# A shared expert's last quarter in units of 512 tokens instead of 256, at other places between the routed experts

## The chip, the cores and the metric

The kernel runs on one core of a Trainium2 chip. The time is the device time of one execution in microseconds, smaller is better: a median of 2704.23 us over three runs (2700.75 to 2708.0). The engines are TensorE (PE, matmuls; PEld, its weight loads), VectorE (DVE), ScalarE (ACT), GpSimd (POOL) and SyncE (SP). SP and POOL issue the DMAs; each engine takes its instructions in a fixed order that was settled when the program was built.

## The reference, cut to what matters

A decoder layer on 4096 tokens of width 512: an attention-like block, a cross attention, then a feed-forward part with one shared expert and 32 routed ones (top 1). Only the last part is touched:

```python
x = hidden_states.reshape(-1, 512)                       # 4096 tokens
shared_out = (silu(x @ shared_gate_w) * (x @ shared_up_w)) @ shared_down_w    # inner width 1024
logits = x @ gate_w                                       # 32 experts
topk_ids = argmax(logits, -1); scores = sigmoid(max(logits, -1))
xs = x * scores
# each token by its own expert e: (silu(xs @ gate[e]) * (xs @ up[e])) @ down[e]
return shared_out + routed_out
```

All is float32. The kernel keeps that precision with split operands: `split` makes a high part (a cast on ScalarE to TensorE's reduced float32) and a low part (the difference, on VectorE unless told otherwise), and every product of two split operands is three matmuls (`three`: low by high, high by low, high by high).

## The kernel before, in words

**Stages.** `build` runs stage0 (first block), stage1 (cross attention, normalisation, gate, the transposed and split tokens `zT` in DRAM), `shared`, `routed` and `overflow` (a loop for experts with more tokens than their place allows; its count is read from the plan). Written in one program, they overlap at their seams: a planner orders each engine's instructions at build time by their place in the program and by a timeline that it computes, gives tiles free buffers of their tag, and adds the waits.

**Shared expert.** Its inner width is 1024. `shared` does the first 768 (three pairs of 256), and writes the sum with the residual plainly to `out`. The last 256 are the class `Rest`, in units of tokens, and stand between the routed experts: a unit's `load` brings its tokens `z` (high and low) from `zT`; `gate` and `up` make the products with the resident weights; `down` makes the outputs, which are copied to a tile `v` and added to `out` by an accumulating DMA from POOL. A unit of 256 tokens has 24 matmuls of 256 columns in gate, 24 in up, and 12 of 512 columns in down.

**Routed experts.** `routed` takes them by rank: `CAP` gives the room of each rank (448, 384, five of 256, four of 192, thirteen of 128, eight of 64 tokens); which expert holds a rank is read at run time from `plan`. An expert's tokens are cut into blocks of 256, 128 and 64. `gather` fetches rows of `xs` by index, `turn` transposes them on TensorE, gate and up are made by `hidden` (256) or `gate`/`up` (128, 64), `down` scatters its outputs with an accumulating indirect DMA (L1331). Each expert has 24 weight pieces of 128 x 512 (eight each for gate, up, down), loaded by SP (L1185) to one of 14 landing buffers (six of tag "raw", eight of tag F, in a fixed cycle) and split (L94 on ACT, L97 on DVE) into tiles of W (45, gate and up) or A and B (eight each, down).

**The order.** The list `blocks` decides. Before the change it begins with shared unit 0, and one further unit follows each expert whose room isn't 128, as long as there are any. With S for shared units and rank:tokens for the routed blocks:

```
S0 0:256 0:128 0:64 S1 24:64 S2 11:128 1:256 1:128 S3 25:64 S4 12:128 2:256 S5 26:64 S6 13:128 3:256 S7
27:64 S8 14:128 4:256 S9 28:64 S10 15:128 5:256 S11 29:64 S12 16:128 6:256 S13 30:64 S14 17:128 7:128 7:64
S15 31:64 18:128 8:128 8:64 19:128 20:128 9:128 9:64 21:128 22:128 10:128 10:64 23:128
```

For block i the loop writes down, in this order: `prepare` of block i+2 (its z or its gather), the next expert's gate weights, the gate of i, the transposes, the next expert's up weights, the up of i, and then the down of block i-1, with the down weights of the expert that follows that block's expert. (For a block of 256, "gate" and "up" are the two halves of `hidden`.) So a block's down stands behind the whole gate and up of the next block. The z of unit 0 is loaded at the end of `shared`.

**Buffers that the change touches.** z: tag E, four tiles, all four for one unit. s: G (four). The split hidden values: C and D (six each). v: I (two). Banks of PSUM: P1 (down, and the transposes of blocks under 256), P2 (gate), P3 (up), P4, two of each.

Of the kernel before, what the change touches and what calls it, by code (L numbers as in the profile page):

```python
# [8 lines left out]
F32 = mybir.dt.float32  # L9
FR = mybir.dt.float32r  # L10
# [4 lines left out]
A = mybir.AluOpType  # L15
AF = mybir.ActivationFunctionType
# [5 lines left out]
T = 4096  # L22
C = 512
E = 32
# [5 lines left out]
CAP = [448, 384] + [256] * 5 + [192] * 4 + [128] * 13 + [64] * 8  # L30
# [11 lines left out]
def f32(ap):  # L42
    return ap.bitcast(F32)
# [45 lines left out]
def split(g, hi, lo, src, lo_engine=None, hi_engine=None):  # L89

    if isinstance(lo_engine, cycle):
        lo_engine = next(lo_engine)
    if hi_engine is None:
        g.nc.scalar.copy(hi, src)  # L94
    else:
        hi_engine.tensor_copy(hi, src)
    g.low = (lo_engine or g.nc.vector).tensor_tensor(lo, src, f32(hi), A.subtract)  # L97
# [22 lines left out]
def part(w, k, c):  # L120

    return w[k][c // 4][:, c % 4 * 128:c % 4 * 128 + 128]
# [40 lines left out]
def three(terms):  # L163

    (wh, wl), (xh, xl) = terms
    return (wl, xh), (wh, xl), (wh, xh)
# [199 lines left out]
def place(t):  # L366

    at = t // 4 * 4 + t % 2 * 2 + t % 4 // 2
    return slice(at * 256, at * 256 + 256)


def stage1(g, x1, mask, kst, vst, gate, x2, zT, zF, xs, ef, background):
    nc = g.nc
    NT = T // 256
# [534 lines left out]
def shared(g, zT, zF, x2, out, pairs, wd, routing, rest, rest_weights):  # L909
# [129 lines left out]
    for n, (G, p) in enumerate(steps):  # L1039
        last = n + 1 == len(steps)  # L1040
        if p == PAIRS - 2 and G + 1 < NG:
            parts = sums(g, zF, G + 1, SUM, nc.gpsimd)
        wn = {}
        ahead = rest_weights if last else pairs.steps(steps[n + 1][1], wn)
        behind = down_weights(g, wd, p, w)
        more = pairs.sums(2) if n == 0 else None

        def between(a):
            next(ahead, None)
            if len(before) < 5:  # L1050
                next(behind, None)
            if parts:
                next(parts, None)
            if p == PAIRS - 1 and G + 1 < NG:
                Z[a] = load_z(g, zT, SUM, G + 1, a, nc.gpsimd)
            if before:
                before.pop(0)()
            if more:
                next(more, None)
            next(routing, None)  # L1060

        up(G, p, w, between)
        while before:
            before.pop(0)()
        for _ in ahead:
            pass
        before = [lambda a=(G, p, w, half, s): down(*a) for half in (1, 0) for s in range(4)]
        w = wn
# [19 lines left out]
class Rest:  # L1088
# [5 lines left out]

    def load(self, b):
        g, nc = self.g, self.g.nc
        z = []
        for c in range(2):
            z.append([])
            for i in range(2):  # L1100
                v = g.tile("E", "z", FR, (128, 2, 256))
                nc.sync.dma_start(f32(v[:]), self.zT[i, :, 2 * c:2 * c + 2, place(b)])
                z[c].append(v)
        self.Z[b] = z

    def product(self, b, which, tag):
        g, nc = self.g, self.g.nc
        p = g.bank(tag, which, (128, 2, 256))
        for i in range(2):
            n = 0  # L1110
            for k in range(4):
                for w, x in three((g.rest[which], self.Z[b][k // 2])):
                    nc.tensor.matmul(p[:, i, :], part(w, k, i), x[:, k % 2, :], start=n == 0, stop=n == 11)
                    n += 1
        return p

    def gate(self, b):
        g, nc = self.g, self.g.nc
        p = self.product(b, "g", "P2")
        s = g.tile("G", "s", F32, (128, 2, 256))  # L1120
        nc.scalar.activation(s[:], p[:], AF.Silu)
        self.S[b] = s

    def up(self, b):
        g, nc = self.g, self.g.nc
        p = self.product(b, "u", "P3")
        s = self.S.pop(b)
        nc.vector.tensor_tensor(s[:], p[:], s[:], A.mult)
        hh, hl = g.tile("C", "hh", FR, (128, 2, 256)), g.tile("D", "hl", FR, (128, 2, 256))
        split(g, hh[:], hl[:], s[:])  # L1130
        self.H[b] = hh, hl
        del self.Z[b]

    def down(self, b):
        g, nc = self.g, self.g.nc
        h = self.H.pop(b)
        for j in range(2):
            o = g.bank("P1", "d")
            n = 0
            for k in range(2):  # L1140
                for w, y in three((g.rest["d"], h)):
                    nc.tensor.matmul(o[:], y[:, k, j * 128:(j + 1) * 128], w[k][0], start=n == 0, stop=n == 5)
                    n += 1
            v = g.tile("I", "v")
            nc.scalar.copy(v[:], o[:])
            nc.gpsimd.dma_start(self.out[b * 256 + j * 128:b * 256 + j * 128 + 128, :], v[:], accum_op=A.add)

def routed(g, xs, rest, plan, idx, wg, wu, wd, out):  # L1150
    nc = g.nc
# [84 lines left out]
    def up_product(b, r, which, tag):  # L1236
        hi, lo = W[r][which]
        for n in range(2):
            p = g.bank(tag, which)
            product(p, [(X[b], k) for k in range(4)], [(hi[2 * k + n], lo[2 * k + n]) for k in range(4)])  # L1240
            yield p
# [90 lines left out]
                                         in_=v[rows], in_offset=None, bounds_check=T - 1, oob_is_err=False, compute_op=A.add)  # L1332


    left = [(b, None, 256) for b in range(T // 256)]
    blocks = [left.pop(0)]
    for r in order:
        at = 0
        while at < CAP[r]:
            m = next(m for m in (256, 128, 64) if at + m <= CAP[r])  # L1340
            blocks.append((BASE[r] + at // 128, r, m))
            at += m
        if CAP[r] != 128 and left:
            blocks.append(left.pop(0))
    blocks += left
    nxt = dict(zip(order, order[1:]))
# [16 lines left out]
    def second(b, r, m):  # L1363
        if r is None:
            rest.up(b)
        elif m < 256:
            up(b, r, m)
        else:
            hidden(b, r, 1)

    def third(b, r, m):
        if r is None:
            rest.down(b)
        else:
            down(b, r, m)
# [13 lines left out]
    for w in "gud":  # L1389
        load(order[0], w)  # L1390
    for i, block in enumerate(blocks):
        b, r, m = block
        last = r is not None and (i + 1 == len(blocks) or blocks[i + 1][1] != r)
        if i + 2 < len(blocks):
            prepare(*blocks[i + 2])
        if last and r in nxt:
            load(nxt[r], "g")
        first(*block)
        if i + 1 < len(blocks):
            turn_x(*blocks[i + 1])  # L1400
        if i > 0:
            turn_hidden(*blocks[i - 1])
        if last and r in nxt:
            load(nxt[r], "u")
        second(*block)
        if i > 0:
            third(*blocks[i - 1])
            r = blocks[i - 1][1]
            if r != block[1] and r in nxt:
                load(nxt[r], "d")  # L1410
# [64 lines left out]
def build(tc, I, out):  # L1475
    from contextlib import ExitStack
    nc = tc.nc
    with ExitStack() as outer:
# [14 lines left out]
        with ExitStack() as inner:  # L1493
            g = Ctx(tc, inner)
            g.ident = ident[:]
            g.mhalf = g.c.tile([128, 8], F32, name="mhalf")
            nc.gpsimd.memset(g.mhalf[:], -0.5)
            ef = g.c.tile([128, E], F32, name="ef")
            idx = g.c.tile([128, NB], I32, name="idx")
            with later(g, 20):  # L1500
                nc.sync.dma_start(ident[:], I["ident"])
                empty = g.tile("A", "empty", I32, (128, NBLK))
                nc.gpsimd.memset(empty[:], T)
                for v in lists:
# [50 lines left out]
```

## Time and profile before

| | |
|---|---|
| median of three runs | 2704.23 us (2700.75 to 2708.0) |
| the profiled execution, time and span | 2703.28 us, 2701.4 us |
| granted TensorE clock, mean over the span | 0.997 |
| busy: PE, DVE, ACT, POOL | 2641.7, 2071.4, 1853.0, 1132.2 us |
| first and last gate matmul of the shared units (L1113) | 1798.3 us, 2472.2 us |
| start of rank 0's first product | 1825.8 us |
| start of the last matmul | 2690.9 us |
| bytes moved by DMA | 446.66 MB |

All places in time are microseconds from the start of the span of one profiled execution. "PE L1113 MATMUL g<-z,rw" is a matmul issued by line 1113 that writes a tile named g from tiles z and rw. Matmuls are pipelined: the duration of one is longer than the distance to the next. In a list of waits a row names the waiting engine and line, what it waited for, and the total, the number and the longest of these waits.

### The profile page before, as it was taken

The numbers are of one execution on the slowest core, as the hardware profiler recorded it, in microseconds if no ns is written. First come the engines' busy times: TensorE is split into PE (matmuls) and PEld (weight loads), VectorE is DVE, ScalarE is ACT, GpSimd is POOL, SyncE is SP. The second block draws the span as 40 slices with busy tenths as digits, with TensorE's granted clock in tenths as the row PEclk, the third lists the DMA queues.
The fourth block names the chain that finished last, engine by engine and source line by source line (L and its number), as shares of the span: only waits on it lengthen the run. The fifth ranks groups of instructions, "written<-read, shape, count | busy, mean of one in ns | idle before, by whom it ended". The sixth has DMA issues, their size and how long they took to land. (4 is left out here: it accounts for less than half of the span.)

```text
span 2701.4 us, 47562 instructions
## 1 busy us (share of the span) xinstructions
PE 2641.7 (98%) x14629; PEld 2274.0 (84%) x14629; DVE 2071.4 (77%) x4703; ACT 1853.0 (69%) x4118; POOL 1132.2 (42%) x911
## 2 busy tenths in 40 slices
PE   7999999999999999999999999999999999999998
PEld 5878888887878999899997878778989898898886
DVE  7777777777777988888887487574777777778985
ACT  7788788888767777677785323343666676767885
POOL 5576565666644334344341457621122222212221
PEclk9999999999999999999999999999999999999999
DMA  4012112212021223323249846663889899999994
GB/s 154 32 63 86 55 67 81 81 47 76 30 87 34 80 76 130 103 92 107 79 143 338 289 142 238 218 211 108 261 282 281 281 305 299 295 284 291 323 319 148
DMA packets 269408, 446.66 MB, mean 165 GB/s; under 512 B 33536, under 2 KB 77568, under 8 KB 269152
## 3 DMA queue, kind: packets, MB, share of 16 engines
q1 hardware_dynamic: 254464, 416.46, 45.5%
q0 software_dynamic: 14688, 27.17, 4.9%
q8 instruction: 115, 1.88, 0.3%
q14 instruction: 141, 1.16, 0.1%
HBM read 348.83 MB, written 96.64 MB: 165 GB/s over the span
## 5 line engine op out<-in xcount | busy, mean ns | idle before, releaser
L97 DVE TENSOR_TENSOR rl<-raw,rh 128x512 fp32r<-128x512 f32 x768 | 487.7, 683 | 86.8 <-ACT rh L94 59.6
L94 ACT CAST rh<-raw 128x512 fp32r<-128x512 f32 x768 | 438.3, 621 | 138.5 <-DMA raw<-in_rg 89.2
L97 POOL TENSOR_TENSOR pl<-p,ph 128x512 fp32r<-128x512 f32 x320 | 411.3, 1296 | 263.2 <-ACT ph L94 206.5
L349 ACT ACTIVATE rl<-s 128x512 f32<-128x512 f32 x512 | 293.0, 604 | 38.1 <-PE s L345 32.8
L1331 POOL DMA_INDIRECT out_dram<-v,idx x46 | 114.7, 2492 | 457.7 <-ACT v L1329 367.4
L464 ACT ACTIVATE e<-e,nm 128x128 f32<-128x128 f32 x512 | 199.2, 391 | 70.4 <-DVE nm L461 70.1
L353 DVE TENSOR_TENSOR p<-s,rl 128x512 f32<-128x512 f32 x320 | 215.0, 682 | 40.6 <-ACT rl L349 38.2
L94 ACT CAST ph<-p 128x512 fp32r<-128x512 f32 x320 | 199.2, 626 | 63.1 <-DVE p L353 60.2
L467 POOL TENSOR_TENSOR e<-e,ri 128x512 f32<-128x512 f32 x128 | 133.2, 1042 | 215.0 <-DVE ri L465 103.3
L345 PE MATMUL s<-qh,kwl 128*128 128x512 f32 x512 | 205.7, 403 | 7.3 <-DVE p L353 4.1
L309 PE MATMUL o<-pl,vwh 128*128 128x512 f32 x512 | 202.8, 396 | 1.4 <-POOL pl L97 1.4
L309 PE MATMUL o<-ph,vwl 128*128 128x512 f32 x512 | 200.4, 393 | 0.9 <-ACT ph L94 0.9
L353 DVE TENSOR_TENSOR s<-s,rl 128x512 f32<-128x512 f32 x192 | 133.2, 694 | 88.3 <-ACT rl L349 87.8
L345 PE MATMUL s<-ql,kwh 128*128 128x512 f32 x512 | 200.1, 391 | 0.0
L345 PE MATMUL s<-qh,kwh 128*128 128x512 f32 x512 | 199.9, 390 | 0.0
L309 PE MATMUL o<-ph,vwh 128*128 128x512 f32 x512 | 199.7, 390 | 0.0
L970 PE MATMUL gu<-z,swh 128*128 128x512 f32 x504 | 157.3, 389 | 0.0
L438 PE MATMUL q<-yh,wql 128*128 128x256 f32 x512 | 149.5, 292 | 2.8 <-DVE v L497 2.4
L97 DVE TENSOR_TENSOR pl<-s,ph 128x512 fp32r<-128x512 f32 x192 | 131.0, 683 | 20.6 <-ACT ph L94 18.2
L438 PE MATMUL q<-yh,wqh 128*128 128x256 f32 x512 | 145.6, 284 | 0.0
L438 PE MATMUL q<-yl,wqh 128*128 128x256 f32 x512 | 145.0, 283 | 0.0
L97 POOL TENSOR_TENSOR vl<-v,vh 128x512 fp32r<-128x512 f32 x64 | 84.4, 1319 | 124.3 <-ACT vh L94 111.6
(361 smaller groups left out, 7996.1 us busy)
## 6 DMA issues: line engine op xcount, KB each, us to landing
raw<-in_rg SPq DMA_DIRECT2D x256, 256.0 KB
raw<-in_ru SPq DMA_DIRECT2D x256, 256.0 KB
raw<-in_rd SPq DMA_DIRECT2D x256, 256.0 KB
z<-zT SPq DMA_DIRECT2D x116, 256.0 KB
b<-x SPq DMA_DIRECT2D x40, 256.0 KB
raw<-in_sgu SPq DMA_DIRECT2D x39, 256.0 KB
swh<-wS SPq DMA_DIRECT2D x36, 256.0 KB
swl<-wS SPq DMA_DIRECT2D x36, 256.0 KB
```

The costliest lines, as they stand in the source:

```text
L94: g.nc.scalar.copy(hi, src)
L97: g.low = (lo_engine or g.nc.vector).tensor_tensor(lo, src, f32(hi), A.subtract)
L309: nc.tensor.matmul(o[:], w, y[:], start=kt == 0 and n == 0, stop=kt == 15 and n == 2)
L345: nc.tensor.matmul(s[:], w, y[:], start=n == 0, stop=n == 2)
L349: m0 = nc.scalar.activation(r[:], s[:], AF.Relu)
L353: m1 = nc.vector.tensor_tensor(p[:], s[:], r[:], A.mult)
L438: nc.tensor.matmul(o[:, i, :], part(w, k, p), y[k // 2][:, k % 2, :], start=n == 0, stop=n == 11)
L464: nc.scalar.activation(e[:, hs], e[:, hs], AF.Exp, bias=nm[:, h:h + 1], scale=0.125, accum_out=su[:, h:h + 1])
L467: nc.gpsimd.tensor_tensor(e4, e4, ri[:].unsqueeze(2).to_broadcast([128, 4, 128]), A.mult)
L970: nc.tensor.matmul(o[:], y, z, start=(at, x) not in begun, stop=j == 1 and m == 2, skip_group_check=True)
L1331: nc.gpsimd.indirect_dma_start(out=out, out_offset=bass.IndirectOffsetOnAxis(ap=idx[rows, b + j:b + j + 1], axis=0), in_=v[rows], in_offse ...
```

## The change

The 4096 tokens go through `Rest` in eight units of 512 instead of sixteen of 256. A unit's z is eight tiles of 128 x 512, four of tag E (high) and four of tag F (low). Gate and up each fill two banks (one for each 128 of the 256 inner columns) with matmuls of 512 columns; each bank has its own Silu, product and split. Down has four outputs of 128 tokens instead of two. The rows of `out` follow from the order in which `zT` holds the tokens. In the list of blocks, a unit follows an expert only if its room is over 128 and under 384, and one unit is always kept back, so that the last block is a shared unit:

```
S0 0:256 0:128 0:64 24:64 11:128 1:256 1:128 25:64 12:128 2:256 S1 26:64 13:128 3:256 S2 27:64 14:128 4:256 S3
28:64 15:128 5:256 S4 29:64 16:128 6:256 S5 30:64 17:128 7:128 7:64 S6 31:64 18:128 8:128 8:64 19:128 20:128
9:128 9:64 21:128 22:128 10:128 10:64 23:128 S7
```

A side effect of the loop's rule for down weights: where a unit stood between two experts, the second one's down weights were asked for with that unit; where it is gone, they are asked for after the gate and up weights of the expert behind.

```diff
     def load(self, b):
-        z = []
-        for c in range(2):
-            z.append([])
+        self.Z[b] = z = []
+        for k in range(4):
+            z.append([g.tile("EF"[i], "z", FR) for i in range(2)])
             for i in range(2):
-                v = g.tile("E", "z", FR, (128, 2, 256))
-                nc.sync.dma_start(f32(v[:]), self.zT[i, :, 2 * c:2 * c + 2, place(b)])
-                z[c].append(v)
-        self.Z[b] = z
+                nc.sync.dma_start(f32(z[k][i][:]), self.zT[i, :, k, b * 512:(b + 1) * 512])
 
     def product(self, b, which, tag):
-        p = g.bank(tag, which, (128, 2, 256))
         for i in range(2):
+            p = g.bank(tag, which)
             n = 0
             for k in range(4):
-                for w, x in three((g.rest[which], self.Z[b][k // 2])):
-                    nc.tensor.matmul(p[:, i, :], part(w, k, i), x[:, k % 2, :], start=n == 0, stop=n == 11)
+                for w, x in three((g.rest[which], self.Z[b][k])):
+                    nc.tensor.matmul(p[:], part(w, k, i), x[:], start=n == 0, stop=n == 11)
                     n += 1
-        return p
+            yield p
 
     def gate(self, b):
-        p = self.product(b, "g", "P2")
-        s = g.tile("G", "s", F32, (128, 2, 256))
-        nc.scalar.activation(s[:], p[:], AF.Silu)
-        self.S[b] = s
+        self.S[b] = []
+        for p in self.product(b, "g", "P2"):
+            s = g.tile("G", "s")
+            nc.scalar.activation(s[:], p[:], AF.Silu)
+            self.S[b].append(s)
 
     def up(self, b):
...
+        for s, p in zip(self.S.pop(b), self.product(b, "u", "P3")):
+            nc.vector.tensor_tensor(s[:], p[:], s[:], A.mult)
+            hh, hl = g.tile("C", "hh", FR), g.tile("D", "hl", FR)
+            split(g, hh[:], hl[:], s[:])
+            self.H[b].append((hh, hl))
 
     def down(self, b):
-        for j in range(2):
+        for s in range(4):
             o = g.bank("P1", "d")
             n = 0
             for k in range(2):
-                for w, y in three((g.rest["d"], h)):
-                    nc.tensor.matmul(o[:], y[:, k, j * 128:(j + 1) * 128], w[k][0], start=n == 0, stop=n == 5)
+                for w, y in three((g.rest["d"], h[k])):
+                    nc.tensor.matmul(o[:], y[:, s * 128:(s + 1) * 128], w[k][0], start=n == 0, stop=n == 5)
                     n += 1
             v = g.tile("I", "v")
             nc.scalar.copy(v[:], o[:])
-            nc.gpsimd.dma_start(self.out[b * 256 + j * 128:b * 256 + j * 128 + 128, :], v[:], accum_op=A.add)
+            at = (b // 2 * 4 + s // 2 * 2 + b % 2) * 256 + s % 2 * 128
+            nc.gpsimd.dma_start(self.out[at:at + 128, :], v[:], accum_op=A.add)
...
-    left = [(b, None, 256) for b in range(T // 256)]
+    left = [(b, None, 512) for b in range(T // 512)]
     blocks = [left.pop(0)]
     for r in order:
...
-        if CAP[r] != 128 and left:
+        if 128 < CAP[r] < 384 and len(left) > 1:
             blocks.append(left.pop(0))
     blocks += left
```

More of the change, by code (lines that the diff above doesn't have):

```diff
@@ L1096, in load @@
         g, nc = self.g, self.g.nc
-        z = []
-        for c in range(2):
-            z.append([])
+        self.Z[b] = z = []
+        for k in range(4):
+            z.append([g.tile("EF"[i], "z", FR) for i in range(2)])
             for i in range(2):
-                v = g.tile("E", "z", FR, (128, 2, 256))
-                nc.sync.dma_start(f32(v[:]), self.zT[i, :, 2 * c:2 * c + 2, place(b)])
-                z[c].append(v)
-        self.Z[b] = z
+                nc.sync.dma_start(f32(z[k][i][:]), self.zT[i, :, k, b * 512:(b + 1) * 512])
     def product(self, b, which, tag):
         g, nc = self.g, self.g.nc
-        p = g.bank(tag, which, (128, 2, 256))
         for i in range(2):
+            p = g.bank(tag, which)
             n = 0
             for k in range(4):
-                for w, x in three((g.rest[which], self.Z[b][k // 2])):
-                    nc.tensor.matmul(p[:, i, :], part(w, k, i), x[:, k % 2, :], start=n == 0, stop=n == 11)
+                for w, x in three((g.rest[which], self.Z[b][k])):
+                    nc.tensor.matmul(p[:], part(w, k, i), x[:], start=n == 0, stop=n == 11)
                     n += 1
-        return p
+            yield p
     def gate(self, b):
         g, nc = self.g, self.g.nc
-        p = self.product(b, "g", "P2")
-        s = g.tile("G", "s", F32, (128, 2, 256))
-        nc.scalar.activation(s[:], p[:], AF.Silu)
-        self.S[b] = s
+        self.S[b] = []
[3 more added lines that the diff above has]
+            self.S[b].append(s)
     def up(self, b):
         g, nc = self.g, self.g.nc
[L1126 to L1131, printed above, removed]
+        self.H[b] = []
+        for s, p in zip(self.S.pop(b), self.product(b, "u", "P3")):
[3 more added lines that the diff above has]
+            self.H[b].append((hh, hl))
         del self.Z[b]
```

## The prediction

> **What bounds the kernel now.** I read the page's engine totals first, then the busy time by stretch for the part that the change touches (from about 1800 us to the end), then TensorE's waits there, its order of time, and last what feeds it. The stretches, one row each: length, busy time of every engine with its instruction count, granted clock, DMA share, GB/s.
>
> ```profile
> PE 2641.7 (98%) x14629; PEld 2274.0 (84%) x14629; DVE 2071.4 (77%) x4703; ACT 1853.0 (69%) x4118; POOL 1132.2 (42%) x911
> ...
> 1900.00:2480.00 580.00, 579.03 (x3517) 517.87 (x3516) 434.31 (x707) 403.90 (x754) 130.98 (x86) 1.00 0.91 286
> 2480.00:2660.00 180.00, 179.66 (x852) 148.33 (x851) 164.11 (x273) 149.34 (x284) 48.38 (x22) 1.00 0.94 316
> ```
>
> TensorE is busy 579.03 of 580 and 179.66 of 180 us. A busy TensorE need not be at its peak, so I look at its waits between 1850 and 2690 us (total, times, longest), which are all of them:
>
> ```profile
> PE g L1288 <- ACT th L94: 1.0, 2, 0.6
> PE d L1233 <- ACT th L94: 0.5, 1, 0.5
> PE d L1142 <- DVE tl L97: 0.3, 1, 0.3
> PE d L1233 <- DVE tl L97: 0.2, 1, 0.2
> ```
>
> Two microseconds in 840, and the clock is 1.00. So in the routed stage the time is the number of matmuls times the distance of their starts. Close behind stand the DMA engines (0.91 to 0.94) and, after 2480 us, VectorE (164 of 180 us). That is narrow enough that I must ask at each moved step whether the weights still come in time.
>
> **Step 1: 512 columns instead of 256 in gate and up.** Per pair of old units the change replaces 96 matmuls of 256 columns by 48 of 512; the 24 down matmuls of 512 columns stay. In all, 768 matmuls of 256 become 384 of 512. Their distance is read from the order of time, not from the mean durations (283 and 390 ns, which overlap):
>
> ```profile
> 2086.09 0.39 PE L1142 MATMUL d<-rdh,hl 128*128 128x512 f32 x1
> 2086.31 0.39 PE L1142 MATMUL d<-rdh,hh 128*128 128x512 f32 x1
> 2086.54 3.04 PE L1113 MATMUL g<-z,rw 128*128 128x256 f32 x24
> 2089.41 0.60 PE L1204 MATMUL pt<-ident,x 128*128 128x128 f32 x4
> ```
>
> 512 columns: starts 0.227 us apart (2086.31 to 2086.54). 256 columns: 24 matmuls start from 2086.54 on and the next operation begins at 2089.41, so 2.87 / 24 = 0.120 us. Before: 768 x 0.120 = 92.2 us; after: 384 x 0.227 = 87.2 us. **Gain 5.0 us.** The Trainium skill speaks against this gain: "TensorE: Matmul & The Clock Gate", section "Back-to-back issue gap", gives N / 2.4 + 2.5 ns, that is 109.2 and 215.8 ns, hence 768 x 0.1092 - 384 x 0.2158 = 1.0 us only. The row shows 120 and 227, further from the rule for the short one, and I take the row; 1.0 us stays as the lower end. Weight loads halve too (768 to 384), but they overlap.
>
> ScalarE, VectorE and the bytes don't change: per 512 tokens there are still two Silu, two products, two splits, four copies and 2 MB of z, now with 2 KB runs. All these are under TensorE's cover.
>
> **Step 2: the end.** Today the last product of expert rank 23 is followed by one copy and one scatter:
>
> ```profile
> 2691.41 0.59 ACT L1329 COPY v<-d 128x512 f32<-128x512 f32 x1 [5.88 <-issue]
> ...
> 2692.27 1.56 POOL L1331 DMA_INDIRECT out_dram<-v,idx  x1 [5.42 <-ACTq L1420]
> ```
>
> The last matmul starts at 2690.94; the scatter's issue ends at 2693.83, 2.9 us later; 7.6 us more to the end of the span at 2701.4. After the change, rank 23's down comes ahead of the last shared unit's down (24 x 0.227 = 5.4 us, four outputs). The accumulating DMA of a shared unit waits until the scatter before it has landed:
>
> ```profile
> 2006.87 1.89 POOL L1146 DMA_DIRECT2D out_dram<-v  x2 [6.78 <-DMA out_dram<-v,idx]
> ```
>
> and v has two buffers (tag I). Counted from M, the start of rank 23's last matmul: copy to M+1.06, scatter issued M+1.33 to 2.89. Landing: M+5.9 (near the 2.9 us that pass at the end of the trace between the scatter's issue and the release at 2696.8; 6.8 after issue when DMA is crowded; "DMA: Bandwidth & Descriptors", section "Anatomy of one DMA - SWDGE (gpsimd) path", would give 2.0 us + 0.6 for 256 KB, nearly the 2.9, so I take 3). Output 0 then goes out at M+6.1 to 7.0; output 1 gets the scatter's buffer at M+5.9, is copied and goes out by M+8.0. Outputs 2 and 3 wait for those buffers: output 0 landed at about M+9.5, copy, issue; output 1 landed at M+10.4, output 3 copied by M+11.0 and issued by M+12.1. Hidden behind matmuls alone it would be M+5.4+2.9 = M+8.3. **Loss 3.8 us** (0 if the order leaves room, 9 with 6.8 us landings). In exchange rank 23's own wait before its down (0.5 + 0.2 in the list, with weight loads 1.2 us) is filled by the last unit's matmuls: **gain 1.2 us**. The four copies also hold ScalarE in order; at the end nothing is behind them.
>
> **Step 3: no shared unit between the early experts.** Two units of 8.5 us (48 x 0.120 + 12 x 0.227) no longer stand around ranks 24 and 11, nor around 1 and 25. From the end of rank 0's last up product to the first product of rank 1, TensorE now has: rank 0's down 5.4 + 3.6, rank 24's gate and up 7.3, rank 11's 10.9, rank 24's down 3.6, transposes 3.3: 34 us instead of the 50 us of the trace (1880 to 1930). By its end 44 weight pieces must be split (24's up and down, 11's gate and up, 1's gate and half its up). In those 50 us:
>
> ```profile
> 1880.00:1930.00 50.00, 50.00 (x281) 43.41 (x280) 41.92 (x71) 38.70 (x75) 11.23 (x9) 1.00 0.98 302
> ...
> L97 DVE TENSOR_TENSOR rl<-raw,rh 128x512 fp32r<-128x512 f32 x49 | 31.2, 683 | 4.0 <-ACT rh L94 3.9
> ```
>
> 49 pieces at a DMA share of 0.98. The fastest that the trace shows over long is the tail (2480 to 2660), which has no shared unit:
>
> ```profile
> L97 DVE TENSOR_TENSOR rl<-raw,rh 128x512 fp32r<-128x512 f32 x205 | 128.8, 681 | 15.0 <-ACT rh L94 14.4
> ```
>
> 205 in 180 us, 0.88 us a piece. 44 x 0.88 = 38.7 us against 34: **4.7 us late**, and TensorE waits that long once (0 if more is prefetched while rank 0 runs its 64 us; 50 x 44/49 - 34 = 11 us at today's pace). What helps: shared z loads no longer compete there, and rank 11's down weights are now asked for after rank 1's gate and up. The next such stretch (25, 12, then 2) has 41 us for 42 pieces, 37 us: in time.
>
> **Step 4: the later stretches and the buffers.** z now takes four of the eight F tiles, which weight pieces also land in (14 buffers in all, six of them "raw"), from two blocks ahead until the unit's up: some 50 of each 80 us. What the queue of weight DMAs waits for today:
>
> ```profile
> SPq L1185 <- DVE rl L97: 234.0, 169, 42.4
> SPq L1102 <- PE u L1113: 35.8, 21, 14.2
> ```
>
> The first row is SP waiting for a buffer: it runs ahead until all are full, so there is slack to lose. The second row, 35.8 us of z loads blocking the queue until the unit before has ended, goes away with units 80 us apart. Ranks 31, 18, 8 follow each other today with one unit of 8.5 us ahead of them and none between, and TensorE loses only the 0.3 us of L1142 there (0.8 counting its weight load); that is the nearest row to 26, 13, 3 after the change. With ten buffers instead of fourteen I take 0.25 us a stretch, six stretches: **1.5 us** (0 to 20). ScalarE meets two waits for a landing in each down (outputs 2 and 3), 3 us each behind which casts queue; TensorE's next need of them is 10.9 us off (two products of the next expert).
>
> **Step 5: the entry.** TensorE waits three times before rank 0 starts:
>
> ```profile
> 1811.87 0.66 PE L1204 MATMUL pt<-ident,x 128*128 128x128 f32 x4 [2.12 <-DMA x<-xs,idx]
> ...
> 1823.80 0.66 PE L1223 MATMUL pt<-ident,x 128*128 128x128 f32 x4 [1.35 <-DVE acc L1008]
> 1825.00 1.11 PE L1223 MATMUL pt<-ident,x 128*128 128x128 f32 x4 [0.55 <-DVE acc L1008]
> ```
>
> About 4.5 us with pipeline restarts. The first unit has 16.3 us of work instead of 8.5, which can stand there; its four accumulating DMAs stand on POOL's queue before gathers of x. Between -4.5 and +2 I take **-1.0 us**.
>
> **Sum**: -5.0 + 3.8 - 1.2 + 4.7 + 1.5 - 1.0 = +2.8 us. On the profiled execution's 2703.28 us (span 2701.4) that is 2706.1; the median of the runs, 2704.23, lies 0.95 above, so **2707 us**. 0.3%, about what a measurement of this kernel can tell from no change, is 8.1 us.
>
> **Rivals.**
> *Weights late in every stretch (slower).* If the four F tiles are missed, each of the stretches with a 64, a 128 and a 256 block (seven after the first) costs about 2.5 us, half of the first one's 4.7. Without step 4 the sum is +1.3; 7 x 2.5 makes +18.8: 2723 us. It decides from 1.0 us a stretch on. For it: the DMA share of 0.98 and VectorE at 91% in the tail. Against it: ranks 31, 18, 8 today.
> *The outputs stay in line (slower).* With 6.8 us landings at the end (+9) and 11 us at the entry to rank 1: -5.0 + 9 - 1.2 + 11 = +13.8, 2718 us. Against it: the DMA engines are nearly idle at the end.
> *All gains, no loss (faster).* -5.0 - 1.2 - 4.5 = -10.7: 2693.5 us; needs rank 24 and 11 fully prefetched and the last outputs not in line.
> *The wider matmul brings only the rule's 1.0 us*: 2711 us, still within.
>
> **How the numbers follow.** Net near zero (likeliest, own range 2697 to 2712): 0.45. Weights late: 0.29; outputs in line: 0.09; together slower 0.38. All gains: 0.17. The range 2693 to 2723 leaves some 0.05 below and 0.15 above.
>
> **What would show it.** Step 1: gate and up of the shared units with 384 matmuls starting 0.227 us apart. Step 2: after the last matmul, copies that wait for the landing of an output, and over 10.5 us from the last matmul to the end. Step 3: one wait of TensorE for a split piece before rank 1's first product. Step 4: TensorE's waits between 2050 and 2480 us stay under 2 us in all. Wrong if these waits repeat for each expert, if the clock falls below 1.00, or if the new order of instructions puts ScalarE's waits ahead of what TensorE needs.

## The result, and the profile after

The changed kernel takes 2718.2 us (median of five runs, 2715.07 to 2721.23; the kernel before, five runs by now, 2704.23). Its ratio to the kernel before is 1.0056, 95% interval 1.0045 to 1.0066: **slower by 0.56%, about 15 us**. The profiled execution has that same time, with a span of 2716.4 us (before: 2703.28 and 2701.4).

The engine totals of the page after:

```profile
PE 2643.5 (97%) x14245; PEld 2256.4 (83%) x14245; DVE 2074.2 (76%) x4703; ACT 1858.9 (68%) x4118; POOL 1129.7 (42%) x911
```

384 matmuls fewer, as the diff says; the rest is as before. The busy time by stretch after (length, then busy time and count of PE, PEld, DVE, ACT, POOL, granted clock, DMA share, GB/s):

```profile
1900.00:2480.00 580.00, 567.65 (x3132) 491.17 (x3131) 442.96 (x716) 411.64 (x761) 124.41 (x81) 1.00 0.91 284
2480.00:2660.00 180.00, 180.00 (x853) 149.28 (x852) 163.24 (x269) 146.91 (x278) 47.10 (x23) 1.00 0.95 318
```

The first row had 579.03 us of TensorE before and has 567.65 now: 11.4 us more of idleness, all of it in the stretch of the routed experts with shared units. The second row lost nothing. TensorE's waits after, from 1850 us to the end, name the place:

```profile
PE d L1232 <- DVE th L97: 10.2, 4, 3.5
PE d L1140 <- ACT v L1143: 2.1, 1, 2.1
PE g L1287 <- ACT th L94: 1.1, 1, 1.1
PE g L1287 <- DVE tl L97: 1.0, 3, 0.4
```

A routed down (L1232) waits four times, 10.2 us in all, for its hidden values to be cast and split (th). The second row is at the end of the work.

For the experiments I also sum, from the trace, by how much each matmul's start is further from the next than its pitch (0.226 us for 512 columns, 0.120 for 256, 0.109 for 128, 0.060 for fewer; positive differences only). I call this TensorE's excess. From the first shared matmul to the end of the span:

```
us                                      before    after   difference
pitch x number of matmuls                874.7    869.3     -5.4
excess up to 1850 (entry)                  6.7      6.9     +0.2
excess 1850 to 2050 (early experts)        2.8      5.2     +2.4
excess 2050 to 2480 (later stretches)      8.0     20.9    +12.9
excess 2480 to the last matmul             5.7      6.0     +0.3
last matmul's start to the end            10.5     14.4     +3.9
span from the first shared matmul        903.1    917.9    +14.8
```

Each column is from one profiled execution, and adds up to some 5 us more than its span, because starts closer than the pitch are left out. The differences add up to 14.3 of the 14.8 us. By far the largest term is the later stretches.

**What stands there.** ScalarE between 2070 and 2087 us, around the outputs of unit S1 (start, duration, line, operation, and the idle time ahead with what ended it):

```profile
2074.19 0.59 ACT L1143 COPY v<-d 128x512 f32<-128x512 f32 x1
...
2079.34 0.62 ACT L94 CAST rh<-raw 128x512 fp32r<-128x512 f32 x1 [2.04 <-DMA raw<-in_rg]
2083.61 0.59 ACT L1143 COPY v<-d 128x512 f32<-128x512 f32 x1 [3.65 <-DMA out_dram<-v]
...
2085.61 0.38 ACT L94 CAST th<-ht 128x256 fp32r<-128x256 f32 x1
```

The last copy of the unit's outputs finds both tiles of v (tag I) still in an accumulating DMA and waits 3.65 us for one to land. ScalarE takes its instructions in order, so the cast of rank 26's transposed hidden values stands behind it, though its input has been there since the transposes of 2077.7 us. Ahead of the copy, ScalarE had already waited 2.04 us for a gate weight piece. TensorE at that place:

```profile
2083.97 0.28 PE L1287 MATMUL g<-th,rl 128*128 128x256 f32 x1
2086.83 0.50 PE L1232 MATMUL d<-rl,th 128*128 128x512 f32 x1 [2.59 <-DVE th L97]
```

The same happens at 2169, 2253 and 2338 us, once for each of the next units (at the first two of these places the copy ahead of the last one waits too, 2.1 and 1.7 us). So two waits meet on ScalarE, one for an output buffer and one for weights. The experiments separate them.

### The profile page after: what moved, and what is told of

The parts are those of the page before. It is cut to its first block, busy times and chain, and to the rows that moved or that the text cites. A ratio compares the mean times of both kernels' runs of the same rounds, so it can differ in the third digit from the quotient of the medians.

```text
span 2716.4 us, 46762 instructions
## 1 busy us (share of the span) xinstructions
PE 2643.5 (97%) x14245; PEld 2256.4 (83%) x14245; DVE 2074.2 (76%) x4703; ACT 1858.9 (68%) x4118; POOL 1129.7 (42%) x911
## 4 chain that ended last, share of the span: by engine, by line
PE 75%; DVE 11%; ACT 5%; DMA 5%; issue 2%; POOL 1%; SPq 0%; POOLq 0%; ACTq 0%; DVEq 0%
PE s L345 12%; PE o L309 12%; PE gu L970 5%; PE d L1232 5%; PE g L1232 5%; PE u L1232 4%; PE q L438 4%; PE u L1287 3%; PE wo L514 3%; PE g L1287 3%; PE d L1322 3%; PE d L1002 3%; ACT e L464 2%; DVE e L458 2%; PE sc L453 2%
## 5 line engine op out<-in xcount | busy, mean ns | idle before, releaser
L94 ACT CAST rh<-raw 128x512 fp32r<-128x512 f32 x768 | 445.2, 622 | 136.1 <-DMA raw<-in_rg 64.5
```

## The experiments

Ratios are to the kernel before, measured beside each run on the same chip; its median was 2701.3 to 2701.9 us there, so it is the ratios, not the medians, that compare with the change's 1.0056. All twelve kernels compute the whole layer. An excess is from one profiled execution of its run.

### 1. The four outputs in another tag

v_in_e: the changed kernel with the outputs in the tiles of tag E (free by then, since the unit's z has been used).

```diff
-            v = g.tile("I", "v")
+            v = g.tile("E", "v")
```

> The changed kernel with one edit: the shared units' output tiles v come from tag E (four tiles, idle between a unit's up and the next unit's z) instead of I (two). Theory A (an output copy that waits on ScalarE for the landing of an earlier output's DMA holds the casts queued behind it, and TensorE waits for those): the 10.2 us of TensorE's waits for the th split in rank 26 to 29's downs go, the last output is issued about 10.2 us after the last matmul of rank 23 starts instead of 14.2, TensorE's 2.1 us wait for a copy at the end goes too; together some -15 us, 2703 us (2700 to 2707). Theory B (the weights come late because z holds four of the fourteen landing buffers): the waits before the downs stay, only the end shortens by 4 to 6 us: 2713 us.

Measured: 2708.12 us, ratio 1.0027 (1.0016 to 1.0038). About half of the loss is gone; the number lies between what the two theories gave. TensorE's waits from 1800 us on (the first row is at the entry):

```profile
PE d L1140 <- ACT hh L94: 2.1, 1, 2.1
PE d L1232 <- DVE th L97: 2.0, 3, 1.0
```

The 10.2 us of waits for th are 2.0, but the excess from 2050 to 2480 us is still 13.4, against 8.0 before the change. In this version SyncE waits for the outputs to leave the tiles before it can bring new z (1850 to 2500 us):

```profile
SPq L1101 <- DMA out_dram<-v: 29.9, 7, 17.5
```

So a second edit put the outputs into C and D, the tiles of the hidden values, to see whether this wait is what remains.

```diff
+            v = g.tile("I" if b == 0 else "CD"[s % 2], "v")
```

> The changed kernel; the shared units' output tiles v come alternately from tags C and D (six each, two of each free at that time) instead of I (two), but for the first unit, which keeps I. Differs from the run with v in tag E in that the next unit's z, which also uses E, doesn't wait for an output's landing (SP's z loads waited 29.9 us for it there). Theory A (ScalarE held by the wait for a landing is the whole loss between 1850 and 2690 us): TensorE's waits and excess there fall to the level of before, some 11 us less than with the change alone and 5 less than with v in E; the end stays 4.5 us longer than before. Ratio to before about 1.000 (0.999 to 1.0015). Theory B (weights late through the F buffers is part of it): no better than with v in E, 1.0027.

Measured: 2709.64 us, ratio 1.0025 (1.0014 to 1.0036), excess 14.4. The same: z being late for tag E was not the rest. A third edit gives only the last output of each unit another tile:

```diff
+            v = g.tile("C" if b > 0 and s == 3 else "I", "v")
```

> The changed kernel; of the four outputs of a unit only the last one's tile v comes from tag C, the other three from I (the first unit keeps I). In the changed kernel's trace the third copy found its tile free at 2074.2 us and the fourth held ScalarE until 2083.6. Theory A: the fourth copy's hold is the loss, so TensorE's 10.2 us of waits before the downs fall to 3 us or less, and the last output at the end goes out about 1 us earlier: ratio to before 1.001 to 1.003. Theory B: they stay, 1.005.

Measured: 2709.67 us, ratio 1.0026 (1.0016 to 1.0036). The waits for th are 3.3 us in all:

```profile
PE d L1232 <- DVE th L97: 3.3, 4, 1.2
```

Moving one copy of four takes as much off the time as moving all: **the fourth copy is the one whose wait costs**. Some 0.3%, 8 us, hang on it when the rest of the change stays. The one trace shows less of it than the median: its excess from 2050 to 2480 us is 17.7, against 13.4 and 14.4 with all copies moved.

### 2. No unit at the end

none_last: all units stand between experts, as the last one before did; rank 23's down ends the work.

```diff
-        if 128 < CAP[r] < 384 and len(left) > 1:
+        if 128 < CAP[r] < 384 and left:
```

> The changed kernel with one edit: no unit is kept back for the end, the last one follows rank 8. The work then ends as before the change, with rank 23's down and one scatter. Theory A: the end is 5.2 us shorter (the four outputs in line cost 6.4 us more than one behind matmuls, the filled wait of rank 23 gives 1.2 back), but rank 8's unit brings one more copy that holds ScalarE, 0 to 3 us: 2713 to 2716 us. If the end were not where the time is lost: 2718 us or more.

Measured: 2709.91 us, ratio 1.0034 (1.0021 to 1.0046): 0.22% or 6 us are won, a little more than the 2 to 5 expected. From the last matmul's start to the end there are again 10.5 us, and the last line of GpSimd is the scatter of before:

```profile
2697.19 1.57 POOL L1330 DMA_INDIRECT out_dram<-v,idx  x1 [5.43 <-ACTq L1420]
```

These 3.9 us are about half of what this execution won. As much lies ahead of the end: the excess from 2050 to 2480 us is 16.5 instead of 20.9, and the waits for th are 5.4 instead of 10.2 us, though the list of blocks is the same there. Why is not shown.

With the outputs in C and D besides:

> The same with no unit kept back for the end; the last follows rank 8. Theory A: 4.5 us less again at the end, 1.2 us back for rank 23's own wait: ratio to before about 0.9985 (0.997 to 1.000), of which the wider matmul's 5.0 us are the gain. If the end isn't where the remaining time is lost, no difference to the run before this one.

Measured: 2708.49 us, ratio 1.0026 (1.0017 to 1.0035): a miss. The two edits together give what the outputs in C and D give alone (1.0025), so their gains overlap, and a third cause, worth 8 us or more, was still unnamed. The waits for th no longer come of copies; ScalarE here, at the same place:

```profile
2079.92 0.62 ACT L94 CAST rh<-raw 128x512 fp32r<-128x512 f32 x1 [3.04 <-DMA raw<-in_rg]
...
2082.45 0.39 ACT L94 CAST th<-ht 128x256 fp32r<-128x256 f32 x1
...
2085.80 0.62 ACT L94 CAST rh<-raw 128x512 fp32r<-128x512 f32 x1 [1.40 <-DMA raw<-in_rg]
2086.33 0.37 ACT L94 CAST th<-ht 128x256 fp32r<-128x256 f32 x1
```

Rank 26's th is two tiles. The cast of the first is 3 us earlier than in the changed kernel (2082.45 against 2085.61), but that of the second hardly is (2086.33 against 2086.91): it now stands behind gate weights that have not landed, and TensorE still waits 1.48 us for it.

### 3. The places alone, and the landing buffers alone

pairs_256: the kernel before, its units of 256 tokens set two and two at the places of the change (the second of the first pair after rank 0), with z in E or F by turns.

```diff
-                v = g.tile("E", "z", FR, (128, 2, 256))
+                v = g.tile("EF"[b % 2], "z", FR, (128, 2, 256))
-        if CAP[r] != 128 and left:
+        if r == 0:
             blocks.append(left.pop(0))
+        if 128 < CAP[r] < 384 and len(left) > 2:
+            blocks += [left.pop(0), left.pop(0)]
```

> The places of the changed kernel with the units of before: two units of 256 tokens at each of its places (the second one's z in tag F), two at the end; each down then has two outputs, for which the two tiles of tag I suffice. Theory A: no copy waits for the landing of an output of its own unit, so the 10.2 us of waits before the downs go; the wider matmul's 5.0 us are lost; the end is 2 us shorter: 2711 us (2707 to 2714). Theory B (the places or the buffers make the weights late): the waits stay and the 5.0 us are lost: 2721 us.

Measured: 2707.85 us, ratio 1.0024 (1.0014 to 1.0034). Its excess from 2050 to 2480 us is 7.5, as before the change and as the first theory had it: **the places themselves cost nothing there**. It also has four F tiles held by z in each of these stretches. But the second unit's z is asked for one block later than in the change, and stands behind rank 13's down weights:

```profile
2086.37 6.41 SPq L1185 DMA_DIRECT2D raw<-in_rd  x8
2093.08 3.54 SPq L1102 DMA_DIRECT2D z<-zT  x4
```

Its tiles are free again at 2144 us, so z in four F tiles for some 51 us, behind the weights, is covered here. What the kernel loses is mainly at the entry (excess 13.0 instead of 6.7), where a gather is late:

```profile
PE pt L1204 <- DMA x<-xs,idx: 4.5, 1, 4.5
```

z_in_f: the kernel before, with all of z in the landing buffers F. That takes four of fourteen from the weights for nearly the whole time.

```diff
-                v = g.tile("E", "z", FR, (128, 2, 256))
+                v = g.tile("F", "z", FR, (128, 2, 256))
```

> The kernel before with one edit: a unit's four z tiles come from tag F, where weight pieces land too, instead of E, which then lies idle. Units of 256 tokens follow each other every 40 us or so, so z holds four of the fourteen landing buffers nearly all the time. Theory A: TensorE's waits stay under 4 us between 1850 and 2480 us, 2704 to 2708 us. Theory B: weights come late in each stretch, 2714 us or more.

Measured: 2727.55 us, ratio 1.0098 (1.0084 to 1.0113), so 26 us for the buffers. TensorE's largest waits are now in the gate products of the routed experts' 256-token blocks (L1288; from 1800 us on):

```profile
PE g L1288 <- ACT th L94: 11.2, 7, 3.9
```

One objection was that the fixed cycle of landing buffers still offers each F tile to the weights in its turn, and that the queue stands at a taken one. z_in_f_cycle takes four of the eight F out of the cycle:

```diff
-    turns = {"u": cycle("W"), "d": cycle("A" * 8 + "B" * 8), "raw": cycle("rFrFFrFrFFrFrF")}
+    turns = {"u": cycle("W"), "d": cycle("A" * 8 + "B" * 8), "raw": cycle("rFrrFrFrrF")}
```

> The kernel before with z in tag F, as in the run that was 26 us slower, and a second edit: the fixed cycle of landing buffers takes six of tag raw and four of F in ten turns instead of six and eight in fourteen. If the loss came from turns that fall to F while only four of its tiles are free, most of it goes: 2712 us or less. If ten buffers are too few whatever the cycle, it stays: 2720 us or more.

Measured: 2729.5 us, ratio 1.0098 (1.0083 to 1.0114). The same time, as the second theory had it, but the traces show two opposite differences in it. Up to 2050 us the excess is 10.8 us instead of z_in_f's 18.5; from 2050 to 2480 us it is the same (22.0 and 21.1), so there the turns don't matter; and behind the last shared unit, where no z is loaded any more, the same 1004 matmuls take 227.4 us, against 218.8 in z_in_f, which has all fourteen buffers back there, and 214.9 before (waits for late weights, and some 10 us at half clock with them). So ten buffers instead of fourteen are too few by themselves, with no z in the queue. Landing buffers held by z are dear: the fear of step 4 was right, and its price was not.

### 4. The second half of z, one block later

In the changed kernel a unit's z is asked for two blocks ahead. SyncE's queue between S1 and S2 (start, duration, what it issues):

```profile
2048.89 2.81 SPq L1101 DMA_DIRECT2D z<-zT  x4
...
2062.67 5.94 SPq L1101 DMA_DIRECT2D z<-zT  x4
2070.81 4.75 SPq L1184 DMA_DIRECT2D raw<-in_rg  x7
2076.20 13.67 SPq L1184 DMA_DIRECT2D raw<-in_ru  x8
```

The first four loads go to E. The other four, at 2062.67, go to F tiles as the weights' splits free them, 1 MB ahead of all but one of rank 3's gate pieces, for a unit whose first product is due at 2121 us. late_z asks for a unit's z one block ahead; x is gathered as before.

```diff
-        if i + 2 < len(blocks):
+        if i + 1 < len(blocks) and blocks[i + 1][1] is None:
+            prepare(*blocks[i + 1])
+        if i + 2 < len(blocks) and blocks[i + 2][1] is not None:
             prepare(*blocks[i + 2])
```

> The changed kernel, but the landing of a wide unit's inputs (2 MB) is asked for one block ahead of the unit instead of two, so the weights of the following narrow expert stand ahead of it in SP's queue. Theory A (part of the loss between 2050 and 2480 us comes of these inputs lying ahead of weights): the excess of that stretch falls from 20.9 us by about 7 to 13-15, ratio to the kernel before about 1.003. Theory B (the order in SP's queue doesn't matter, the loss is in the fourth copy and in the places alone): excess 19-22, ratio 1.005-1.006. If the inputs now come too late for the unit itself, TensorE waits at the unit's first gate matmuls (L1103 z or its product), and the ratio is above 1.0056.

Measured: 2707.04 us, ratio 1.0022 (1.0015 to 1.003). The time is a little better than expected; the excess fell less, to 16.6, but the profiled execution was a slow one of its kind (2712.01 us), and 3.2 us of its excess are two stretches at half clock (last section), where the change's 20.9 has one. With the outputs in C and D and no unit at the end besides:

> The changed kernel with three edits together: the output copies of the down steps of all but the first 512-token unit go to buffers C and D, no unit ends the work (all are at places between experts), and the inputs of a unit are asked for one block ahead. Theory A (the three causes add): excess from 2050 to 2480 us falls to about 8, as in the kernel before; the end is as before (10.5 us after the last matmul); what is left is the gain of the wide matmul (5 us), so the ratio is 0.998-0.9995. Theory B (the remaining loss is not from the order of the loads): the excess stays at 13-16 us and the ratio at 1.002-1.003, as with the first two edits alone (1.0026).

Measured: 2697.87 us, ratio 0.9988 (0.9982 to 0.9995), excess 6.7. **With all three edits the wide units are faster than the kernel before.** Two last runs complete the table of the three edits, and show which of them are needed:

> The changed kernel with the inputs of a wide unit asked for one block ahead and the output copies of the later units' downs in buffers C and D; the last unit still ends the work. Against the version with the unit at a place between experts as well (0.9988), this shows the price of the end. Theory A (the end costs what the traces' ends show, 4 to 6 us): ratio to the kernel before 1.000-1.001, TensorE's excess from 2050 to 2480 us at 6-9, and 14-15.5 us from the last matmul to the end of the span. Theory B (the end costs nothing once the stretch before it keeps its rate): ratio 0.9985-0.9992.

> The changed kernel with the inputs of a wide unit asked for one block ahead and no unit at the end of the work; the four output copies stay in the two buffers of tag I. Against the version with the copies in C and D as well (0.9988), this shows the price of the fourth copy. Theory A (the held copy costs 3 to 8 us in the stretches whatever the order of the loads): ratio 1.000-1.002, excess from 2050 to 2480 us at 10-15. Theory B (the held copy only cost time because the gate and up casts behind it were late already; with the weights early it is covered): ratio 0.9985-0.9993, excess 6-9.

Measured: late_z_v_cd_end 2696.74 us, 0.9981 (0.9975 to 0.9988), excess 6.7, 14.5 us from the last matmul to the end; late_z_none_last 2703.95 us, 1.0008 (1.0001 to 1.0015), excess 14.2. All eight together (the change itself is the upper left one):

```
ratio to the kernel before        z two blocks ahead   z one block ahead
outputs in I,    unit at the end        1.0056              1.0022
outputs in I,    no unit at the end     1.0034              1.0008
outputs in C/D,  unit at the end        1.0025              0.9981
outputs in C/D,  no unit at the end     1.0026              0.9988
```

Each interval is about 0.1% to either side. Reading across, z later brings 0.26 to 0.44% in every row, 7 to 12 us. Reading down with a unit at the end, the outputs in C and D bring 0.31 and 0.41%; with none, 0.08 (not told from nothing) and 0.20%, so the first theory of late_z_none_last held: the held copy costs something even when the weights come first. The unit at the end costs 0.22 and 0.14% if its outputs share two tiles (at the edge of the intervals), and nothing if they don't (0.9981 against 0.9988, in the end's favour, with intervals that overlap). So the first theory of late_z_v_cd_end, that the end costs 4 to 6 us in any case, fell: what the last outputs cost after the last matmul comes back ahead of it, where rank 23's own waits are covered (excess from 2480 us to the last matmul 3.0 against 7.8 without the unit). **Two causes account for the loss: four outputs in two tiles, and z asked for too early.**

The best version keeps the change's order of work and its last unit. SyncE's queue in it:

```profile
2048.91 2.55 SPq L1101 DMA_DIRECT2D z<-zT  x4
...
2062.28 7.53 SPq L1184 DMA_DIRECT2D raw<-in_rg  x8
2070.80 5.57 SPq L1184 DMA_DIRECT2D raw<-in_ru  x8
2076.63 10.67 SPq L1184 DMA_DIRECT2D raw<-in_rd  x8
2087.74 2.90 SPq L1101 DMA_DIRECT2D z<-zT  x4
```

Half of z leaves 25 us later, behind rank 3's gate and up and rank 13's down weights; gate starts where z stood, and up is through by 2076.4 instead of 2089.9 us. The other half hasn't moved. In this version the list of TensorE's waits from 1850 us to the end has no row at all, and the stretch is full:

```profile
2050.00:2480.00 430.00, 430.00 (x2336) 371.01 (x2335) 336.82 (x544) 315.75 (x586) 89.04 (x68) 1.00 0.94 296
```

The same row of the changed kernel:

```profile
2050.00:2480.00 430.00, 419.11 (x2268) 360.60 (x2267) 322.87 (x519) 303.23 (x560) 85.55 (x63) 1.00 0.93 285
```

**What stays open.** Later z does two things: the weights go first, and each F tile is held for some 40 us (2087.7 to 2128) instead of 70 (2062.7 to 2132). z_in_f and z_in_f_cycle show that missing tiles cost, v_cd_none_last shows late gate weights, and pairs_256 that a hold of 51 us behind the weights is covered, but no run changed the order in the queue without the holding time. The shares of the two are not told apart. Nor were such edits tried on the kernel before, so that the best version's gain is that of the wider matmuls rests on the count in step 1 below.

## Why the prediction was partly right, step by step

The forecast was 2707 us with a range from 2693 to 2723; the measured 2718.2 lies inside the range, outside the likeliest case's own range (2697 to 2712), on the slower side that had a chance of 0.38. That it lies inside is owed to the width that the range was given for late weights: the sum of the steps was +2.8 us, the profiles differ by 14.8. The forecast's own sign of being wrong came, waits that repeat for each expert: from 2050 to 2480 us they are 10.9 us, not under 2.

**Step 1, the wide matmuls: right.** Predicted -5.0 us. From each start to the next, the matmuls of gate and up in the shared units take 94.0 us before (768) and 88.6 us after (384): -5.4. The pitch of 512 columns holds; after, in the order of time,

```profile
2678.72 4.02 PE L1110 MATMUL g<-z,rw 128*128 128x512 f32 x17
2682.58 1.03 PE L1203 MATMUL ht<-ident,s 128*128 128x128 f32 x8
```

17 matmuls in 3.86 us, 0.227 us each. The 1.0 us by the issue-gap rule that was weighed there was too little; the section cited with it gives it for the gap of an isolated matmul, not for a stream with weight loads as here. The best version's gain of 5.1 us (0.19% of 2701.88) is about this step's.

**Step 2, the end: mechanism right, size short by some 2 us.** Predicted +3.8 and -1.2, together +2.6. Measured +4.2: after the last matmul there are 3.9 us more than before, and ahead of it 0.3, because TensorE waits 2.1 us for a copy (the second row of its waits), which the prediction did not have. GpSimd after:

```profile
2695.45 1.56 POOL L1330 DMA_INDIRECT out_dram<-v,idx  x1 [14.89 <-ACT v L1328]
2700.51 1.89 POOL L1145 DMA_DIRECT2D out_dram<-v  x2 [3.50 <-DMA out_dram<-v,idx]
2705.76 0.86 POOL L1145 DMA_DIRECT2D out_dram<-v  x1 [3.36 <-ACT v L1143]
2707.46 0.86 POOL L1145 DMA_DIRECT2D out_dram<-v  x1 [0.83 <-ACTq L1420]
```

With M at 2694.1 us, the scatter is issued M+1.35 to M+2.9 (predicted 1.33 to 2.89), the first outputs go at M+6.4 (6.1), the last is issued by M+14.2 (12.1): the landings of outputs 0 and 1 took longer than assumed. In the prediction's own count that is a loss of 5.9 instead of 3.8. The measured excess shows rank 23's own wait filled where the copies don't hold TensorE: 0.2 us over the last 25 us in v_in_e against 1.5 before, the predicted 1.2 or so.

**Step 3, the early stretch: wrong.** It gave +4.7 us; no wait stands ahead of rank 1's first product at 1920.8 us, and the whole early part lost 2.4. The stretch itself took 33 us (1888 to 1921), as counted. VectorE's split pieces in it:

```profile
L97 DVE TENSOR_TENSOR rl<-raw,rh 128x512 fp32r<-128x512 f32 x39 | 24.6, 679 | 0.1
```

39 pieces in 33 us are 0.85 us each, hardly better than the 0.88 I took. What failed is the count of 44 as due by its end. None of them was split ahead: by 1888 us VectorE had done 30 routed pieces, rank 0's 24 and six of rank 24's gate (told apart by the order of loads and splits). When rank 1's first product started it had done 68, and ScalarE, through with rank 1's gate, stood waiting for its up:

```profile
1920.81 0.36 PE L1287 MATMUL g<-th,rl 128*128 128x256 f32 x1
1921.08 0.62 ACT L94 CAST rh<-raw 128x512 fp32r<-128x512 f32 x1 [0.57 <-DMA raw<-in_ru]
```

So 36 of the 44 were enough. The product takes its pieces one after the other: the last four of the gate were split by 1924.0 us, while it ran, and its first up matmul came at 1928.2. With the two pieces left of rank 24's gate, 38 x 0.88 = 33 us is in time.

**Step 4, the later stretches: the step that failed.** It gave +1.5 us; measured +12.9. Two sentences of it were wrong.

- "TensorE's next need of them is 10.9 us off" counted only weights behind the held copies. Behind them stood also the casts of the hidden values of the expert between (th of rank 26), which TensorE needs some 6 us after their transposes (2077.7 to 2084.0), whatever the weights do. The copies' wait of 3 us was well guessed: this one was 3.65.
- "that is the nearest row to 26, 13, 3 after the change": the stretch 31, 18, 8 has no z loaded within it. The row stood for the places, and for these it was right (pairs_256). It could not stand for 1 MB of z in the landing buffers and ahead of the weights. The holding time was taken as some 50 of each 80 us; it was some 70.

The rows from which I concluded on slack misled too. After the change (1850 to 2500 us):

```profile
SPq L1184 <- DVE rl L97: 240.8, 186, 45.0
SPq L1184 <- PE u L1110: 24.1, 13, 4.7
```

The first row is 240.1 us before, in the same stretch. SyncE waits as long for free buffers as ever, while weights come late: a queue that waits for buffers may be ahead, or may have too few of them, and the row does not say which. The 35.8 us of z loads waiting for the unit before are gone, as forecast. The second row stands in their place: weights (L1184) that wait for an F tile until a unit's up has used the z in it.

**Step 5, the entry: no gain.** Predicted -1.0, measured +0.2. The three old waits are gone, and the unit's own come in their place (TensorE's waits from 1800 to 1850 us, after):

```profile
PE d L1140 <- ACT hh L94: 2.3, 2, 1.4
```

**The rivals.** "Weights late in every stretch" (2723 us, from 1.0 us a stretch on) was nearest: 12.9 us over the later stretches. It had the F tiles right and the copies missing. "The outputs stay in line" gave 2718 us, the measured time, but by luck: it named the end and the entry to rank 1; the outputs did stay in line, but between the experts. The new order of instructions putting ScalarE's waits ahead of what TensorE needs was in the list of what would make the prediction wrong, without a price.

## What to carry to other kernels

When a unit doubles, count what it hands in at once: four outputs through two buffers make an in-order engine wait, and the price is what stands behind that copy in its program order, hidden values as well as weights. A prefetch is not free because it is early: it takes landing buffers and queue places from what is needed sooner, so ask for it as late as its use allows. Test such causes together as well as one at a time, since here single edits won back 0.2 to 0.3% each, two could bring no more than one, and only with the outputs and the loads both mended did a gain like the wide matmul's own appear.

## What the runs showed of the hardware

A wait of TensorE can cost more than itself. After the 2.59 us of waiting before 2086.83 us in the changed kernel, the starts of the 512-column matmuls lie 0.43 us apart for a while:

```profile
2088.10 0.61 PE L1232 MATMUL d<-rh,th 128*128 128x512 f32 x1
2088.50 0.63 PE L1232 MATMUL d<-rl,th 128*128 128x512 f32 x1
2088.93 0.63 PE L1232 MATMUL d<-rh,th 128*128 128x512 f32 x1
...
2091.49 0.41 PE L1232 MATMUL d<-rh,th 128*128 128x512 f32 x1
```

The granted clock by stretch there:

```profile
2087.00:2090.00 3.00, 3.00 (x10) 2.39 (x11) 3.00 (x6) 1.86 (x5) 0.00 (x0) 0.68 0.80 195
```

The 0.68 is the mean of 1.1 us at full clock and 1.9 us at half. From 2088.10 to 2091.49 us, 3.4 us at half pace, which adds 1.6 us to the wait. The Trainium skill ("TensorE: Matmul & The Clock Gate", "Part 1: The HAM clock gate") describes a clock that halves after an idle window of 3.4 us and takes a busy window of the same length to return; the length agrees, though here waiting of less than 3 us was enough. Of the four waits for th only this one was followed by it, so it is 1.6 of the 12.9 us, and none of my steps had it. The length of the wait does not decide it: in the change one of 3.46 us (2257 us) was not followed by it, in late_z waits of 1.98 and 1.94 us (2084 and 2333 us) were.
